# Half of a normalised input brought in transposed and scaled by GpSimd, in a gated feed-forward kernel

## The chip, the cores and the metric

The kernel runs on one core of a Trainium2 chip. The metric is the device time of one launch in microseconds; less is better. All data are fp32.

## The reference

The input has 2 x 1024 = 2048 tokens of 512 features. It is layer-normalised once, and the result goes through two branches:

```python
xn = (x - mean) / sqrt(var + 1e-5)                 # per token
s  = xn @ (weight * (block mask > 0)).T            # 512 -> 512, mask by blocks of 32 x 32
nx = xn * rsqrt(mean(xn**2) + 1e-5) * ln_w         # per token, per feature
f  = (silu(nx @ gate_w.T) * (nx @ up_w.T)) @ down_w.T   # 512 -> 1792 -> 512
out = x + s * silu(f)
```

## The kernel before, in words

**Layout.** The kernel works on transposed data: features on the 128 partitions, 512 tokens (a token tile, t = 0 to 3) on the free axis. The normalised input is thus a grid of blocks (c, t), with c = 0 to 3 the block of 128 features. All large tiles are slots of 128x512 in one SBUF tensor `mem`; `RINGS` gives names to stretches of it (B1 to B7, v5, tmp, free and so on), and `F` their first slots.

**Fast matrix products, twice nested.** The grid is split in two by two (K is the half of the features, H the half of the tokens), and each such block again in two by two (k, n). Both levels use a Winograd-like scheme with seven products in place of eight. An outer product q needs sums or differences of outer blocks: `outer_b` makes them for q = 5, 6, 7 and 4 (for 1, 2 and 3 a block is used as it is). `inner_b` makes the same sums within the blocks of q. On the side of the weights `inner_a` does it on GpSimd. An instance j is one outer product of one group of weights g (seven groups of gate and up columns, and an eighth for the masked linear); it consists of seven inner products m, each a matmul of 128x128x512 that PE runs as two records. An instance starts at position 7j of the order.

**Banks.** The products of an instance accumulate in PSUM banks x, y and z, and the running sum of a bank is read between two products of the same bank (`snap` and `total`, DVE for the instances with a prior, ACT for many of the others). Of instance j, DVE's read `total x` stands at position 7j + 9, and the product m=4, which goes on in the same bank x, at 7j + 12.

**The order.** Nothing is scheduled by a tool. Each step is put in a list with a position, `at(pos, fn, ...)`; the list is sorted by position and issued under a manual schedule, so that every engine works through its own share of it in that order. One position is about the length of one product. The first 16 instances (positions 0 to 112) are q = 1 and 2 of all groups, which need only the first token half (t = 0 and 1). From position 112 on the instances use the other five outer products, which need the second half too. The blocks of the second half are therefore made ready beside the running instances, at positions 40 to 118.

**The second half before.** Token tiles 2 and 3 are loaded with tokens on the partitions. `stats` and `factors` give for each token a scale and a shift (`scl`, `nb`). `normalise` applies them in place, four times on ACT for t = 2 and four times on DVE for t = 3. Then PE transposes them, for each (t, c) four 128x128 transposes into one bank of the ring V. For c = 2 and 3 ACT copies the bank to SBUF (`evacuate`); for c = 0 and 1 `outer_b` reads the bank itself, once for q = 5 and once for q = 7. `outer_b` for q = 6 and `inner_b` read two SBUF tiles. The subtractions of `outer_b` are on DVE, except those for q = 4, which are on GpSimd (POOL).

**What else runs there.** `mask_rows` are four reductions on DVE at positions 62 to 72.5. DVE multiplies gate and up values (`h_out`), ACT evaluates silu. POOL makes the weight sums `inner_a(g, 1)` of group g at position 14g − 7 and the following three; group 6 has its products m=5, 6, 3 and 7 at positions 86, 88, 90 and 92. The queue of SP issues nearly all transfers, in the order of the list. The factors of the RMS norm already go through a small tensor in DRAM: `rms_store` transposes them with PE, copies them, and stores them with one transfer; `rms_rows` later loads each row of 512 tokens, broadcast to 128 partitions.

Of the kernel before, what the change touches and what calls it, by code (L numbers as in the profile page):

```python
# [8 lines left out]
F32 = mybir.dt.float32  # L9
I32 = mybir.dt.int32  # L10
AF = mybir.ActivationFunctionType
ALU = mybir.AluOpType
AX = mybir.AxisListType

P = 128
W = 512
# [15 lines left out]
def tile_masked_linear_gated_ffn(  # L32
# [11 lines left out]
    nc = tc.nc  # L44
    NT, H = x.shape
    KC = H // P
    G = gu.shape[0]
    NTT = NT // W
    TT = W // P
# [2 lines left out]
    h_dram = tc.dram_tile([7, G, 2, P, W], F32, name="h_dram")  # L52
    s_dram = tc.dram_tile([KC, NTT, P, W], F32, name="s_dram")
    rms_dram = tc.dram_tile([NT], F32, name="rms_dram")
    acc_dram = tc.dram_tile([G + 1, P, 4, W], F32, name="acc_dram")
    dw_dram = tc.dram_tile([4, P, G, 256], F32, name="dw_dram")

    const = ctx.enter_context(tc.tile_pool(name="const", bufs=1))
    small = ctx.enter_context(tc.tile_pool(name="small", bufs=2))
# [8 lines left out]
    def at(pos, fn, *args):  # L68
        events.append((pos, len(events), fn, args))
# [5 lines left out]
    mem = big.tile([P, sum(n for _, n in RINGS), W], F32, tag="mem", name="mem")  # L75
# [5 lines left out]
    F = first_slot  # L81

    def slot(tag, name=None):
        i, n = ring[tag]
        ring[tag][0] += 1
        return mem[:, first_slot[tag] + i % n, :]
# [6 lines left out]
    def bank(tag, name):  # L93
        return ps.tile([P, W], F32, tag=tag, name=name, bufs=PSB[tag])

    def add(eng, o, a, b, op=ALU.add):
        eng.tensor_tensor(o, a, b, op)  # L97

    dve, pool, act = nc.vector, nc.gpsimd, nc.scalar
# [3 lines left out]
    ident = const.tile([P, P], F32, tag="ident", name="ident")  # L103
# [9 lines left out]

    xt, raw, stat = {}, {}, {}
    agg = small.tile([P, NTT, TT, 2], F32, tag="agg", name="agg", bufs=1)
    rms = small.tile([P, NTT, TT], F32, tag="rms", name="rms", bufs=1)

    def load_x(t):
# [10 lines left out]
    def factors(t):  # L129


        scl = small.tile([P, TT], F32, tag="scl", name=f"scl_{t}")
        nb = small.tile([P, TT], F32, tag="nb", name=f"nb_{t}")
        stat[t] = (scl, nb)

        def last():
            nc.vector.reciprocal(scl, scl)
            nc.vector.scalar_tensor_tensor(nb, agg[:, t, :, 0], -1.0, scl, ALU.mult, ALU.mult)

        return [lambda: nc.vector.tensor_scalar(scl, agg[:, t, :, 1], 1.0 + EPS, EPS * EPS, ALU.mult, ALU.add),  # L140
                lambda: nc.scalar.activation(scl, scl, AF.Sqrt), last]
# [8 lines left out]
    pt = {}  # L150
# [17 lines left out]
    def rms_factor():  # L168

        def first():  # L170
            nc.vector.tensor_scalar_add(rms, agg[:, :, :, 1], EPS)
            nc.vector.reciprocal(rms, rms)
            nc.vector.tensor_mul(rms, agg[:, :, :, 1], rms)
            nc.vector.tensor_scalar_add(rms, rms, EPS)
        return [first, lambda: nc.scalar.activation(rms, rms, AF.Sqrt)]

    def rms_store():

        b = bank("V", "rms_rows")
        nc.tensor.transpose(b[: NTT * TT, :P], rms.rearrange("p t i -> p (t i)"), ident)  # L180
        rows = small.tile([NTT * TT, P], F32, tag="rms_rows", name="rms_rows", bufs=1)
        nc.vector.tensor_copy(rows, b[: NTT * TT, :P])
        nc.sync.dma_start(rms_dram.rearrange("(i p) -> i p", p=P), rows)

# [4 lines left out]
        nc.sync.dma_start(rms_bc[t], rms_dram[t * W : (t + 1) * W].unsqueeze(0).to_broadcast([P, W]))  # L189


    bblk, bop = {}, {}

    def outer_b(q, k, n, eng):


        B = lambda K, H_: pt[2 + n, k] if (K, H_) == (0, 1) else raw[2 * K + k, 2 * H_ + n]
        if q in (1, 2, 3):
            bblk[q, k, n] = B(*{1: (0, 0), 2: (1, 0), 3: (1, 1)}[q])
            return  # L200
        o = mem[:, F["free"], :] if (q, k, n) == (4, 0, 1) else slot("tmp" if (k, n) == (0, 1) else f"B{q}")
        a, b = {
            5: lambda: (B(0, 1), B(0, 0)),
            6: lambda: (B(1, 1), bblk[5, k, n]),
            7: lambda: (B(1, 1), B(0, 1)),
            4: lambda: (B(1, 0), bblk[6, k, n]),
        }[q]()
        add(eng, o, a, b, ALU.subtract)
        bblk[q, k, n] = o
# [274 lines left out]
    K3 = G // 2  # L484
# [55 lines left out]
    def first_h(q, k, i5, i7):  # L540

        st = {}

        def in_bank():
            st[0] = bank("V", f"h_{k}")
            nc.scalar.copy(st[0], dh[q][:, 1, k, :])

        def sums():
            for m, i in ((5, i5), (7, i7)):
                dt.setdefault((q, m), slots(i, K3))  # L550
            add(dve, dt[q, 5][:, k, :], st[0], dh[q][:, 0, k, :], ALU.subtract)
            add(dve, dt[q, 7][:, k, :], dh[q][:, 1, K3 + k, :], st[0], ALU.subtract)

        return in_bank, sums
# [119 lines left out]
    where = {gq: j for j, gq in enumerate(order)}  # L674
    N = len(order)
    END = 7 * N
# [16 lines left out]
    def plan(pos, step, todo):  # L693
        for i, fn in enumerate(todo):
            at(pos + step * i, fn)
# [32 lines left out]
    for i in range(TT):  # L728
        at(14.0 + 2.5 * i, stats, 2, i)
        at(25.0 + 3 * i, stats, 3, i)  # L730
        at((44.0, 51.0, 55.2, 58.2)[i], normalise, 2, i, act)
        at(40.5 + 2.4 * i, normalise, 3, i, dve)
    plan(36.2, 1.2, rms_factor())

    for t, p0 in ((3, 51.5), (2, 65.5)):
        n = t % 2
        for k, c in enumerate((2, 3, 0, 1)):
            for i in range(TT):
                at(p0 + 2 * k + 0.01 * i, transpose, t, c, i, "V")
            if c >= 2:  # L740
                at(p0 + 2 * k + 1.2, evacuate, t, c, act)
            else:
                at(p0 + 2 * k + 1.2, outer_b, 5, c, n, dve)
                at(p0 + 2 * k + 1.21, outer_b, 7, c, n, dve)
    for k in (0, 1):
        for n in (0, 1):
            at(72, outer_b, 3, k, n, None)
    for n, p0 in ((1, 60), (0, 74)):
        for k in (0, 1):
            at(p0 + 1.5 * k, outer_b, 6, k, n, dve)  # L750
            at(p0 + 2.2 + 1.7 * k + (16 if n == 1 else 4), outer_b, 4, k, n, pool)
    for q, p in ((6, 77), (5, 83), (4, 89), (7, 100), (3, 118)):
        for off, m, eng in ((0, 5, dve), (3, 6, dve), (5.5, 7, pool), (7.5, 4, pool)):
            at(p + off, inner_b, q, m, eng)

# [2 lines left out]
    for g in range(G + 1):  # L758
        p, rest = 7 * where[g, 1], 7 * where[g, BLOCKS[0]]
# [40 lines left out]
    free = [p for p in range(END, END + 25 * 7 + 20) if p not in taken]  # L800
    DOWN = (1, 2, 6, 5, 7, 3, 4)

    def D(o):
        return lambda k: free[25 * o + k] if 25 * o + k < 25 * len(DOWN) else free[25 * o + k - 1] + 1
# [1 line left out]
    H0, H1 = F["B1"], F["B6"]  # L806
    TS = [F["B7"] + K3 * k for k in range(5)]
    first_t = {5: F["q"] - 1, 7: F["vc"], 6: F["a1"], 4: TS[1]}
    b11, b12, b21, b22, e0, e1 = (0, 0, K3), (1, 0, K3), (0, K3, 2 * K3), (1, K3, 2 * K3), (0, G - 1, G), (1, G - 1, G)
    QD, later = (F["a1"] + 4, F["acc"], F["s"] + 5), {}  # L810
    for o, q in enumerate(DOWN):
        if o == 0:
            parts = [(p, 7 * where[min(k, 4) + 1, 6] + 11) for k, p in enumerate((b11, b12, b22, b21, e0, e1))]
        elif o == 1:
            parts = [(p, END - 22 + 7 * p[0]) for p in (b11, b21, e0, b12, b22, e1)]
        else:
            d = D(o - 2)
            parts = [(b11, d(4)), (b12, d(4) + 0.1), (b21, d(14)), (b22, d(21)), (e0, d(25) + 1), (e1, d(25) + 1.1)]
        for part, pos in parts:
            at(pos, load_h, q, (H0, H1)[o % 2], part)  # L820
        for k, m in enumerate((5, 6, 7, 4)):
            if o:
                at(D(o - 1)((3, 8, 12, 18)[k]) + 0.3, inner_h, q, m, TS[(4 * o + k + 3) % 5])
            elif m in (6, 4):
                at(END + {6: -1.95, 4: 7.5}[m], inner_h, q, m, first_t[m])
        if o == 0:
            for k in range(K3):
                in_bank, sums = first_h(q, k, first_t[5], first_t[7])
                at(END - 24.4 + 7 * k, in_bank)
                at(END - 22.95 + 7 * k, sums)  # L830
        at((END - 29.8, END - 14, END + 7)[o] if o < 3 else D(o - 2)(4), load_d, q, QD[o % 3])

        def weight_sums(q=q, i=F["q"] + 2 - 3 * (o % 2), o=o):
            for k, fn in enumerate(inner_d(q, i)):
                later[o, k] = fn
        for k in range(4):
            pos = END + (-6, -4.8, 2, 4)[k] if o == 0 else D(o - 1)(10) + 2.5 * k
            if k == 0:
                at(pos, weight_sums)
            at(pos, lambda o=o, k=k: later[o, k]())  # L840
# [81 lines left out]
```

## Time and profile before

| | us |
|---|---|
| time, median of 3 runs | 514.32 (514.15 to 514.35) |
| profiled execution, its own time | 514.33 |
| span of its profile | 512.5 |
| busy in that span: PE, DVE, POOL, ACT | 506.2, 380.8, 340.5, 181.7 |
| 128x512 on DVE, a PSUM and an SBUF operand | 0.68 each |
| 128x512 on POOL, two SBUF operands | 1.27 each |
| granted clock of PE | 1.0 |

The span is the time from the first to the last recorded instruction; 1.8 us of the execution lie around it. A row of a timeline gives the start and the length in us, the engine, the line of the kernel, the operation, out<-in, and how many instructions were merged in it; in brackets stands how long the engine had been idle, and what ended that. PEld is the weight load, which runs ahead of its matmul. Line 97 is the helper `add`, through which all sums and differences go. Consecutive DVE instructions of 128x512 start 0.60 us apart.

### The profile page before, as it was taken

The numbers are of one execution on the slowest core, as the hardware profiler recorded it, in microseconds if no ns is written. First come the engines' busy times: TensorE is split into PE (matmuls) and PEld (weight loads), VectorE is DVE, ScalarE is ACT, GpSimd is POOL, SyncE is SP. The second block draws the span as 40 slices with busy tenths as digits, with TensorE's granted clock in tenths as the row PEclk, the third lists the DMA queues.
The fourth block names the chain that finished last, engine by engine and source line by source line (L and its number), as shares of the span: only waits on it lengthen the run. The fifth ranks groups of instructions, "written<-read, shape, count | busy, mean of one in ns | idle before, by whom it ended". The sixth has DMA issues, their size and how long they took to land. (4 is left out here: it accounts for less than half of the span.)

```text
span 512.5 us, 4939 instructions
## 1 busy us (share of the span) xinstructions
PE 506.2 (99%) x1277; PEld 231.2 (45%) x1277; DVE 380.8 (74%) x586; ACT 181.7 (35%) x344; POOL 340.5 (66%) x282
## 2 busy tenths in 40 slices
PE   8999999999999999999999999999999999999997
PEld 7444444444444444444444444444444444444444
DVE  5879689875987969789696978968847645367736
ACT  3566864642536344353634433331100101001111
POOL 5522223994695978869598789977652664739960
PEclk9999999999999999999999999999999999999999
DMA  8335645359159486685948567499997698467372
GB/s 310 142 123 215 245 156 217 153 226 329 60 220 334 165 297 233 230 299 209 315 181 296 205 246 258 156 334 390 352 345 269 198 382 320 146 255 220 145 230 83
DMA packets 60460, 121.59 MB, mean 237 GB/s; under 512 B 5760, under 2 KB 13328, under 8 KB 58384
## 3 DMA queue, kind: packets, MB, share of 16 engines
q1 hardware_dynamic: 60144, 120.75, 66.1%
q10 hardware_dynamic: 288, 0.52, 0.3%
q8 instruction: 10, 0.16, 0.1%
q14 instruction: 18, 0.15, 0.1%
HBM read 75.11 MB, written 46.15 MB: 237 GB/s over the span
## 5 line engine op out<-in xcount | busy, mean ns | idle before, releaser
L97 POOL TENSOR_TENSOR mem<-mem 128x512 f32<-128x512 f32 (+4 forms) x245 | 305.8, 1270 | 136.7 <-ACT mem L264 37.6
L343 PE MATMUL x<-mem 128*128 128x512 f32 x448 | 213.6, 594 | 0.3
L343 PEld LDWEIGHTS x<-mem 128*128 128x128 f32 x448 | 83.7, 190 | 106.9 <-issue 86.7
L97 DVE TENSOR_TENSOR mem<-x,mem 128x512 f32<-128x512 f32 x137 | 92.6, 684 | 42.2 <-PE x L343 41.1
L343 PE MATMUL y<-mem 128*128 128x512 f32 x224 | 114.6, 593 | 0.7 <-DVE mem L97 0.7
L97 DVE TENSOR_TENSOR mem<-mem 128x512 f32<-128x512 f32 (+3 forms) x60 | 75.6, 1266 | 7.2 <-PE dx L591 4.4
L591 PE MATMUL dx<-mem 128*128 128x512 f32 x174 | 78.3, 592 | 0.0
L97 DVE TENSOR_TENSOR mem<-y,mem 128x512 f32<-128x512 f32 x96 | 65.7, 684 | 10.0 <-PE y L343 8.7
L343 PEld LDWEIGHTS y<-mem 128*128 128x128 f32 x224 | 42.2, 190 | 53.3 <-issue 46.7
L350 ACT COPY z<-x 128x512 f32<-128x512 f32 x54 | 30.9, 573 | 97.8 <-PE x L343 93.3
L343 PE MATMUL z<-mem 128*128 128x512 f32 x112 | 57.1, 593 | 0.0
L591 PEld LDWEIGHTS dx<-mem 128*128 128x128 f32 x174 | 33.1, 190 | 41.6 <-issue 40.9
L591 PE MATMUL dy<-mem 128*128 128x512 f32 x98 | 44.5, 592 | 0.0
L409 ACT ACTIVATE gate<-mem 128x512 f32<-128x512 f32 x56 | 33.1, 601 | 25.4 <-DVE mem L97 21.0
L414 DVE TENSOR_TENSOR mem<-gate,mem 128x512 f32<-128x512 f32 x56 | 38.1, 681 | 5.1 <-POOL mem L97 4.3
L564 POOL TENSOR_TENSOR mem<-mem 128x512 f32<-128x512 f32 x16 | 24.3, 1516 | 15.4 <-DMA mem<-s_dram 15.1
L343 PEld LDWEIGHTS z<-mem 128*128 128x128 f32 x112 | 21.0, 190 | 25.3 <-issue 24.4
L574 ACT ACTIVATE silu<-mem 128x512 f32<-128x512 f32 x15 | 9.0, 602 | 64.6 <-DVE mem L97 48.3
L97 DVE TENSOR_TENSOR mem<-z,mem 128x512 f32<-128x512 f32 x41 | 28.0, 682 | 3.4 <-PE z L343 3.4
L591 PEld LDWEIGHTS dy<-mem 128*128 128x128 f32 x98 | 18.6, 190 | 23.4 <-issue 23.2
L97 DVE TENSOR_TENSOR mem<-dx,mem 128x512 f32<-128x512 f32 x16 | 11.0, 690 | 20.1 <-PE dx L591 20.1
L591 PE MATMUL dz<-mem 128*128 128x512 f32 x56 | 25.2, 592 | 0.0
(72 smaller groups left out, 286.8 us busy)
## 6 DMA issues: line engine op xcount, KB each, us to landing
h_dram<-mem SPq DMA_DIRECT2D x98, 256.0 KB, 2.1
mem<-h_dram SPq DMA_DIRECT2D x28, 768.0 KB, 6.7
mem<-in_gu SPq DMA_DIRECT2D x42, 256.0 KB, 4.0
acc_dram<-mem SPq DMA_DIRECT2D x8, 1024.0 KB, 4.1
mem<-acc_dram SPq DMA_DIRECT2D x8, 1024.0 KB, 6.0
s_dram<-mem SPq DMA_DIRECT2D x16, 256.0 KB, 4.4
mem<-s_dram SPq DMA_DIRECT2D x16, 256.0 KB, 6.7
mem<-in_x_t SPq DMA_DIRECT2D x16, 256.0 KB, 6.4
```

The costliest lines, as they stand in the source:

```text
L97: eng.tensor_tensor(o, a, b, op)
L343: nc.tensor.matmul(st[key], weights(g, q, m), operand(q, m), start=first and not (key == "z" and seeded), stop=True, skip_group_check=True)
L350: nc.scalar.copy(st["z"], st["x"])
L409: nc.scalar.activation(gate[key], t(), AF.Silu)
L414: nc.vector.tensor_mul(a(), gate[key], b())
L564: at_later.append(lambda: nc.gpsimd.tensor_tensor(s_tile, s_tile, rms_bc[t], ALU.mult))
L574: nc.scalar.activation(b[0][:, part], y[:, part] if source is None else source(), AF.Silu)
L591: nc.tensor.matmul(st[key], w(), b(), start=first and key != "z", stop=True, skip_group_check=True)
```

## The change

Token tiles 2 and 3 are loaded a second time, now from the transposed copy of the input in DRAM (`x_t`), so that features lie on the partitions at once (`load_xt`, eight transfers). Their scale and shift then vary along the free axis. So the factors of both tiles are gathered in one small tile `fac`, transposed once by PE, stored in a small DRAM tensor (`fac_rows`), and loaded back as four rows that are broadcast to 128 partitions (`fac_load`). POOL multiplies each of the eight blocks by the scale row and adds the shift row, in place (`scale_xt`, 16 instructions). The 32 transposes, the eight `normalise` and the four `evacuate` of the second half go. The subtractions `outer_b` for q = 5 and 7 now read two SBUF tiles. Positions of `outer_b` and `inner_b` change, and some slots.

```diff
+    fac_dram = tc.dram_tile([NT], F32, name="fac_dram")
...
+    fac = small.tile([P, 2, 2, TT], F32, tag="fac", name="fac", bufs=1)
...
+        if t < 2:
+            scl = small.tile([P, TT], F32, tag="scl", name=f"scl_{t}")
+            nb = small.tile([P, TT], F32, tag="nb", name=f"nb_{t}")
+        else:
+            scl, nb = fac[:, t - 2, 0, :], fac[:, t - 2, 1, :]
...
+    def load_xt(t, c):
+        K, k, n = c // 2, c % 2, t % 2
+        v = mem[:, F["v5"] + 4 + 2 * n + k, :] if K == 0 else slot("tmp" if (k, n) == (0, 1) else "B3")
+        (b12 if K == 0 else raw)[(k, n) if K == 0 else (c, t)] = v
+        nc.sync.dma_start(v, x_t[c * P : (c + 1) * P, t * W : (t + 1) * W])
+
+    def fac_rows():
+        b = bank("V", "fac_rows")
+        nc.tensor.transpose(b[: 4 * TT, :P], fac.rearrange("p t f i -> p (t f i)"), ident)
+        rows = small.tile([4 * TT, P], F32, tag="rows", name="fac_sb")
+        nc.vector.tensor_copy(rows, b[: 4 * TT, :P])
+        nc.sync.dma_start(fac_dram.rearrange("(i p) -> i p", p=P), rows)
+
+    def fac_load(t):
+        for f in range(2):
+            i = 2 * (t - 2) + f
+            fac_bc[t, f] = mem[:, F["B6"] + 3 + i, :]
+            nc.sync.dma_start(fac_bc[t, f], fac_dram[i * W : (i + 1) * W].unsqueeze(0).to_broadcast([P, W]))
+
+    def scale_xt(t, c, f):
+        v = b12[c, t % 2] if c < 2 else raw[c, t]
+        add(pool, v, v, fac_bc[t, f], (ALU.mult, ALU.add)[f])
...
-        B = lambda K, H_: pt[2 + n, k] if (K, H_) == (0, 1) else raw[2 * K + k, 2 * H_ + n]
+        B = lambda K, H_: b12[k, n] if (K, H_) == (0, 1) else raw[2 * K + k, 2 * H_ + n]
...
-        at((44.0, 51.0, 55.2, 58.2)[i], normalise, 2, i, act)
-        at(40.5 + 2.4 * i, normalise, 3, i, dve)
...
-    for t, p0 in ((3, 51.5), (2, 65.5)):
-        n = t % 2
-        for k, c in enumerate((2, 3, 0, 1)):
-            for i in range(TT):
-                at(p0 + 2 * k + 0.01 * i, transpose, t, c, i, "V")
-            if c >= 2:
-                at(p0 + 2 * k + 1.2, evacuate, t, c, act)
-            else:
-                at(p0 + 2 * k + 1.2, outer_b, 5, c, n, dve)
-                at(p0 + 2 * k + 1.21, outer_b, 7, c, n, dve)
+    for k, (t, c) in enumerate((t, c) for t in (3, 2) for c in range(KC)):
+        at(21.0 + 2 * k, load_xt, t, c)
+        for f in range(2):
+            at((53.5 if t == 3 else 67.5) + 3 * c + 1.5 * f, scale_xt, t, c, f)
+    at(41, fac_rows)
+    for t in (3, 2):
+        at(41.5, fac_load, t)
...
-    for n, p0 in ((1, 60), (0, 74)):
-        for k in (0, 1):
-            at(p0 + 1.5 * k, outer_b, 6, k, n, dve)
-            at(p0 + 2.2 + 1.7 * k + (16 if n == 1 else 4), outer_b, 4, k, n, pool)
-    for q, p in ((6, 77), (5, 83), (4, 89), (7, 100), (3, 118)):
+    for n, p0 in ((1, 61.05), (0, 75.05)):
+        for off, q, k in ((0, 5, 0), (0.01, 5, 1), (7, 7, 0), (7.01, 6, 0), (9.25, 7, 1), (10.25, 6, 1)):
+            at(p0 + off, outer_b, q, k, n, dve)
+        for k in (0, 1):
+            at(p0 + 11.5 + 1.5 * k, outer_b, 4, k, n, pool)
+    for q, p in ((6, 88), (5, 94), (7, 102), (4, 110), (3, 120)):
         for off, m, eng in ((0, 5, dve), (3, 6, dve), (5.5, 7, pool), (7.5, 4, pool)):
             at(p + off, inner_b, q, m, eng)
```

More of the change, by code (lines that the diff above doesn't have):

```diff
@@ L129, in factors @@
     def factors(t):
-        scl = small.tile([P, TT], F32, tag="scl", name=f"scl_{t}")
-        nb = small.tile([P, TT], F32, tag="nb", name=f"nb_{t}")
+        if t < 2:
[3 more added lines that the diff above has]
+            scl, nb = fac[:, t - 2, 0, :], fac[:, t - 2, 1, :]
         stat[t] = (scl, nb)
@@ L180, in rms_store @@
         nc.tensor.transpose(b[: NTT * TT, :P], rms.rearrange("p t i -> p (t i)"), ident)
-        rows = small.tile([NTT * TT, P], F32, tag="rms_rows", name="rms_rows", bufs=1)
+        rows = small.tile([NTT * TT, P], F32, tag="rows", name="rms_rows")
         nc.vector.tensor_copy(rows, b[: NTT * TT, :P])
@@ L189, in rms_rows @@
         nc.sync.dma_start(rms_bc[t], rms_dram[t * W : (t + 1) * W].unsqueeze(0).to_broadcast([P, W]))
+    b12, fac_bc = {}, {}
+    def load_xt(t, c):
[17 more added lines that the diff above has]
+        add(pool, v, v, fac_bc[t, f], (ALU.mult, ALU.add)[f])
     bblk, bop = {}, {}
     def outer_b(q, k, n, eng):
-        B = lambda K, H_: pt[2 + n, k] if (K, H_) == (0, 1) else raw[2 * K + k, 2 * H_ + n]
+        B = lambda K, H_: b12[k, n] if (K, H_) == (0, 1) else raw[2 * K + k, 2 * H_ + n]
         if q in (1, 2, 3):
@@ L200, in outer_b @@
             return
-        o = mem[:, F["free"], :] if (q, k, n) == (4, 0, 1) else slot("tmp" if (k, n) == (0, 1) else f"B{q}")
+        o = mem[:, F["v5"] + 8, :] if (q, k, n) == (4, 0, 1) else slot("tmp" if (k, n) == (0, 1) else f"B{q}")
         a, b = {
@@ L730, in tile_masked_linear_gated_ffn @@
         at(25.0 + 3 * i, stats, 3, i)
-        at((44.0, 51.0, 55.2, 58.2)[i], normalise, 2, i, act)
-        at(40.5 + 2.4 * i, normalise, 3, i, dve)
     plan(36.2, 1.2, rms_factor())
-    for t, p0 in ((3, 51.5), (2, 65.5)):
-        n = t % 2
-        for k, c in enumerate((2, 3, 0, 1)):
-            for i in range(TT):
-                at(p0 + 2 * k + 0.01 * i, transpose, t, c, i, "V")
-            if c >= 2:
-                at(p0 + 2 * k + 1.2, evacuate, t, c, act)
-            else:
-                at(p0 + 2 * k + 1.2, outer_b, 5, c, n, dve)
-                at(p0 + 2 * k + 1.21, outer_b, 7, c, n, dve)
+    for k, (t, c) in enumerate((t, c) for t in (3, 2) for c in range(KC)):
[5 more added lines that the diff above has]
+        at(41.5, fac_load, t)
     for k in (0, 1):
         for n in (0, 1):
-            at(72, outer_b, 3, k, n, None)
-    for n, p0 in ((1, 60), (0, 74)):
+            at(82, outer_b, 3, k, n, None)
+    for n, p0 in ((1, 61.05), (0, 75.05)):
+        for off, q, k in ((0, 5, 0), (0.01, 5, 1), (7, 7, 0), (7.01, 6, 0), (9.25, 7, 1), (10.25, 6, 1)):
+            at(p0 + off, outer_b, q, k, n, dve)
         for k in (0, 1):
-            at(p0 + 1.5 * k, outer_b, 6, k, n, dve)
-            at(p0 + 2.2 + 1.7 * k + (16 if n == 1 else 4), outer_b, 4, k, n, pool)
-    for q, p in ((6, 77), (5, 83), (4, 89), (7, 100), (3, 118)):
+            at(p0 + 11.5 + 1.5 * k, outer_b, 4, k, n, pool)
+    for q, p in ((6, 88), (5, 94), (7, 102), (4, 110), (3, 120)):
         for off, m, eng in ((0, 5, dve), (3, 6, dve), (5.5, 7, pool), (7.5, 4, pool)):
@@ L808, in tile_masked_linear_gated_ffn @@
     first_t = {5: F["q"] - 1, 7: F["vc"], 6: F["a1"], 4: TS[1]}
-    b11, b12, b21, b22, e0, e1 = (0, 0, K3), (1, 0, K3), (0, K3, 2 * K3), (1, K3, 2 * K3), (0, G - 1, G), (1, G - 1, G)
+    p11, p12, p21, p22, e0, e1 = (0, 0, K3), (1, 0, K3), (0, K3, 2 * K3), (1, K3, 2 * K3), (0, G - 1, G), (1, G - 1, G)
     QD, later = (F["a1"] + 4, F["acc"], F["s"] + 5), {}
@@ L812, in tile_masked_linear_gated_ffn @@
         if o == 0:
-            parts = [(p, 7 * where[min(k, 4) + 1, 6] + 11) for k, p in enumerate((b11, b12, b22, b21, e0, e1))]
+            parts = [(p, 7 * where[min(k, 4) + 1, 6] + 11) for k, p in enumerate((p11, p12, p22, p21, e0, e1))]
         elif o == 1:
-            parts = [(p, END - 22 + 7 * p[0]) for p in (b11, b21, e0, b12, b22, e1)]
+            parts = [(p, END - 22 + 7 * p[0]) for p in (p11, p21, e0, p12, p22, e1)]
         else:
             d = D(o - 2)
-            parts = [(b11, d(4)), (b12, d(4) + 0.1), (b21, d(14)), (b22, d(21)), (e0, d(25) + 1), (e1, d(25) + 1.1)]
+            parts = [(p11, d(4)), (p12, d(4) + 0.1), (p21, d(14)), (p22, d(21)), (e0, d(25) + 1), (e1, d(25) + 1.1)]
         for part, pos in parts:
```

## The prediction

> **What bounds the kernel now.** I read the page first: busy time by engine, then the slices, then the busy time in ten-microsecond windows, then the timelines of the stage that the change touches.
>
> ```profile
> PE 506.2 (99%) x1277; PEld 231.2 (45%) x1277; DVE 380.8 (74%) x586; ACT 181.7 (35%) x344; POOL 340.5 (66%) x282
> ```
>
> TensorE (PE) is busy for 506 of 512.5 us. From 30 us on it has next to no idle time, so work taken off PE shortens the run one for one, provided that no other engine becomes late for it. The windows show who has room where the change works (columns: PE, PEld, DVE, ACT, POOL busy us):
>
> ```profile
> 50.00:60.00 10.00, 10.00 (x28) 4.62 (x27) 7.43 (x13) 8.68 (x16) 1.64 (x3) 1.00 0.57 217
> 60.00:70.00 10.00, 10.00 (x33) 4.97 (x32) 7.72 (x13) 6.72 (x13) 1.24 (x2) 1.00 0.64 238
> 70.00:80.00 10.00, 10.00 (x37) 5.18 (x36) 8.04 (x14) 4.45 (x9) 2.88 (x4) 1.00 0.47 169
> 80.00:90.00 10.00, 10.00 (x26) 4.58 (x25) 9.80 (x18) 4.93 (x10) 5.12 (x6) 1.00 0.55 191
> 90.00:100.00 10.00, 10.00 (x25) 4.42 (x24) 8.45 (x13) 6.03 (x14) 10.00 (x8) 1.00 0.46 184
> ```
>
> GpSimd (POOL) has some 20 us of idle time between 50 and 85 us. VectorE (DVE) has not: 8 of 10 us, then 9.8. The price of the transposes is in PE's timeline:
>
> ```profile
> 52.87 1.02 PE L343 MATMUL z<-mem 128*128 128x512 f32 x2
> ...
> 58.02 1.02 PE L343 MATMUL y<-mem 128*128 128x512 f32 x2
> 58.88 0.60 PE L155 MATMUL pt<-ident,mem 128*128 128x128 f32 x4
> 59.31 1.02 PE L343 MATMUL z<-mem 128*128 128x512 f32 x2
> ```
>
> From 58.02 to 58.88 is one product (two records, 0.858 us), from 58.88 to 59.31 four transposes: 0.43 us. The z product at 52.87 stands at position 45 of the written order, so without the later transposes position p falls at 14.26 + 0.858 p us.
>
> What decides the case is a pair of rows further on, where POOL is busy while DVE subtracts two SBUF tiles (POOL's rows each from a window of its own):
>
> ```profile
> 86.29 1.27 POOL L97 TENSOR_TENSOR mem<-mem 128x512 f32<-128x512 f32 x1
> 87.52 1.18 POOL L97 TENSOR_TENSOR mem<-mem 128x256 f32<-128x256 f32 x1
> ...
> 86.93 1.17 DVE L97 TENSOR_TENSOR mem<-mem 128x512 f32<-128x512 f32 x1
> 88.03 0.68 DVE L97 TENSOR_TENSOR mem<-y,mem 128x512 f32<-128x512 f32 x1
> ```
>
> DVE's subtraction takes 1.17 us in place of 0.68: it ends at 88.10, so it really ran from 87.42, when POOL's instruction ended. POOL's next one takes 1.18 in place of 0.73: it waited 0.45 us. I looked up the five such DVE instructions between 86 and 98 us: each time POOL pays about 0.45 us (0.73 to 1.18 twice, 1.27 to 1.78, 1.72 and 1.73), and DVE waits for the end of POOL's current instruction (0.49, 0, 0, 0.53 and 0.29 us). The row with a PSUM operand (y) takes 0.68 whatever POOL does.
>
> **What the Trainium skill says.** SBUF — State Buffer, "Who interferes with whom": a VectorE instruction with two SBUF inputs contends with a GpSimd instruction that reads SBUF, and the later one is blocked for the whole instruction; one with at most one SBUF input does not. The five cases above agree. GPSIMD Engine Reference, "Performance versus the Vector engine": a two-input fp32 elementwise operation takes GpSimd about twice as long as VectorE. The trace agrees: 1.27 against 0.68 us.
>
> **The change, part by part.**
>
> PE: 32 transposes go, eight sets of 0.43 us: −3.44. One transpose of the factors is added; its twin for rms_rows has 128 columns like the others, so 0.43/4 = +0.11. It stands at position 41 (49.4 us), its input is ready at 48.96 (end of the last L138 row); its weight load wants it some 0.25 us ahead, so 0 to 0.3 of wait; I take +0.15. PE net: −3.2.
>
> ACT loses four normalisations (0.8 each) and four PSUM copies (0.59). It was not late; counted at nothing, and scale_a of group 4 comes 0.8 us sooner, so POOL is free at 60.3 instead of 61.2.
>
> DVE loses four normalisations (0.54) near 50 us, gains one copy (0.28). The eight subtractions that read a transposed bank, and the four for q=6, remain, but now all twelve have **two SBUF inputs**.
>
> SP and DMA: eight x_t loads of 256 KB at positions 21 to 35 (about 32 to 45 us), where the DMA share is 0.22 to 0.64; needed after 60 us, so free. The factor rows: copy done about 50.5, store 2.1 (as the h_dram stores) to 3.4 us (as rms_dram), four loads issued 0.32 apart, landing 3.4 to 6.3 us later (as mem<-rms_dram). The first two are there at 56 to 60.5 us, POOL wants them at 60.3 and 61.6: just hidden. SP waits for the store up to 3.4 us; behind it stand an acc_dram store and an h_dram store whose buffers are wanted a round later, and two gu loads, wanted 5 us after they land. Free.
>
> POOL gains 16 instructions of 128x512 (1.23 apart, 1.35 where one waits for its predecessor): 16 x 1.23 + 5 x 0.12 = 20.3 us. By length they fit into the idle time. They also keep POOL busy without a gap from 60.3 to past 95 us, and that is the cost: every outer subtraction of DVE now meets a running POOL.
>
> Follow DVE around position 72 (instance 9). In the trace it reads bank x at 75.01 (position 68); five transpose sets lay before that, so now 75.01 − 2.15 + 0.11 = 72.97. The queue behind it is now: q=7, q=6, mask_rows, total y, q=7, q=6, and then the read of x at position 72. The last product of this instance (m=4) accumulates into the same bank and must wait for that read; it starts at 82.13 − 3.44 + 0.11 = 78.8. A subtraction directly behind another waits for one POOL instruction between them: 1.23 + 0.45 = 1.68 from start to start. Let w be the wait of the first of each pair:
> 72.97 + 0.60 + w + 1.68 + 0.60 + 0.60 + 0.60 + w + 1.68 + 0.60 + 0.68 = 80.0 + 2w.
> With w from 0 to 1.23 I take the middle, 0.6, since POOL now runs without gaps (the five cases above had 0 to 0.53). The bank is free at 81.2; PE wants it at 78.55 (0.25 ahead). Stall: 2.7 us (1.5 to 3.9). Before, the same read ended at 80.0 for a product at 82.1: 2 us in hand.
>
> The second half repeats it at position 82 to 89 without the mask: the product at position 81 starts at 14.26 + 0.858 x 81 + 0.11 = 83.87, DVE reads x 1.06 later as in the trace, at 84.93 + 2.7; then 0.60 + w + 1.68 + 0.60 + 0.60 + w + 1.68 + 0.60 + 0.68: free at 94.1 + 2w, wanted at 90.5 + 2.7 = 93.2. Stall 0.9 + 1.2 = 2.1 us (0.9 to 3.4). Its first operands come from POOL: 17 instructions, 4 sums and ten waits of 0.45 put the last scaled tile near 90, in time for it. The pairs at positions 61 and 75 have the reads of later products behind them with 2 us in hand: I add 0.3.
>
> The inner_b steps go 2 to 21 positions later, on DVE and POOL, and two of the four POOL outer_b earlier. Their first result is wanted by the product at position 114; POOL's queue from 90 us on (two outer_b, two masks, eight inner_b, eight weight sums, 25 us) ends at 115, where it ended at 118 before. Counted at nothing; without that cover each microsecond would be one of PE.
>
> Sum: −3.44 + 0.11 + 0.15 + 2.7 + 2.1 + 0.3 = +1.9. From 105 us on the order is as before and PE is busy, so nothing is given back. The profiled execution took 514.33 us (span 512.5 and 1.8 around it), 0.01 from the median: **516.2 us**.
>
> **The rivals.**
> - *Only POOL pays* (the subtractions slip in between POOL's instructions, w near 0 and no wait within pairs). Then DVE is in time, but POOL's sums for group 6 (wanted at position 86, 88.1 less 0.25) come after 17 x 1.23 + 0.6 + 5 x 0.7 + 10 x 0.45 from 60.3, at 89.8: stall 1.9. 514.33 − 3.2 + 1.9 = 513.0. For it: two of the five cases did not wait. Against: pairs stand back to back. 0.15.
> - *All hidden*, the other side: POOL's idle 20 us take the 20.3 us and DVE's 2 us in hand absorb the waits. 514.33 − 3.2 = 511.1. It decides if the summed waits of DVE's four subtractions stay below about 1.3 us. Against: five of five cases. 0.13.
> - *Rows late*: DRAM rows land after 62 us; each microsecond moves POOL's whole chain and, through operands that DVE waits for, the second stall: about 517.5 to 518.5. For it: the four rms_dram loads took up to 6.3 us. 0.07.
> - That the transposes stay is excluded by the diff.
>
> **How the numbers follow.** The forecast has 0.65, with its own range 514.8 to 518.2 (w between its ends, in both rounds not at once). What can be told from no change is 0.2%, 1.03 us. Faster: all hidden 0.13 and half of "only POOL" 0.07: 0.20. Same: the other half 0.08 and the foot of the forecast 0.06: 0.14. Slower: 0.59 + 0.07 = 0.66. The range leaves out "all hidden" and the top: 512.2 to 518.2.
>
> **What would show it.** PE's busy time falls by about 3.3 us in the sum of its instructions while idle time of 4 to 5 us appears between 76 and 95 us, put down to DVE as the releaser of x products; DVE mem<-mem rows near 1.2 us and POOL rows near 1.7 in that stretch. The forecast is wrong if DVE's subtractions stay at 0.68 beside a busy POOL, if PE has no gap there, or if the gaps are released by POOL or a DMA.

## The result, and the profile after

| | before | after |
|---|---|---|
| time, median of 6 runs each, us | 514.21 (513.99 to 514.35) | 515.99 (515.67 to 516.42) |
| ratio after to before, 95% interval | | 1.0035 (1.0024 to 1.0046) |
| span of the profile, us | 512.5 | 514.2 |
| TensorE, from its first steady z product to its last matmul, us | 479.96 | 480.47 |
| from DVE's last instruction to the end of the span, us | 2.62 | 3.89 |

The changed kernel is 1.8 us slower; 516.2 was forecast. The last two rows split the loss: 0.51 us of it lies in TensorE's stream, and 1.27 us after the last arithmetic, where the forecast had nothing. (In the two profiles the first steady product also comes 0.17 us earlier after the change. Some expectations below have 3.93 and 1.35 us for these ends; they were worked out with spans rounded to 0.1 us.)

In the profile of the changed kernel `add` is line 98, the products of the instances are line 374, and the stores of the output line 609. Its page has this line of busy time:

```profile
PE 504.5 (98%) x1246; PEld 228.4 (44%) x1246; DVE 385.2 (75%) x583; ACT 176.2 (34%) x336; POOL 368.4 (72%) x298
```

PE has 31 instructions fewer and POOL 16 more. DVE has three instructions fewer and is busy 4.4 us longer: its instructions became longer. Busy time in ten-microsecond windows (PE, PEld, DVE, ACT, POOL) shows where:

```profile
60.00:70.00 10.00, 10.00 (x25) 4.39 (x24) 7.68 (x11) 6.02 (x12) 9.77 (x8) 1.00 1.02 394
70.00:80.00 10.00, 9.21 (x22) 3.89 (x21) 9.95 (x15) 4.31 (x9) 9.83 (x9) 1.00 0.34 137
80.00:90.00 10.00, 10.00 (x25) 4.24 (x24) 10.00 (x15) 2.88 (x6) 9.93 (x8) 1.00 0.58 186
90.00:100.00 10.00, 8.47 (x20) 3.37 (x19) 9.34 (x14) 5.53 (x12) 9.84 (x9) 1.00 0.44 176
```

Between 60 and 90 us POOL went from 1 to 5 us of each window to nearly all of it (from 90 us on it was full before too), DVE is nearly full from 70 us on, and PE, full before, has gaps between 70 and 80 and between 90 and 100 us. They lie at these products (PE's timeline of the changed kernel):

```profile
76.84 1.02 PE L374 MATMUL z<-mem 128*128 128x512 f32 x2
77.70 1.02 PE L374 MATMUL x<-mem 128*128 128x512 f32 x2
79.51 1.12 PE L374 MATMUL x<-mem 128*128 128x512 f32 x2 [0.79 <-DVE mem L98]
80.48 1.02 PE L374 MATMUL y<-mem 128*128 128x512 f32 x2
...
90.53 1.02 PE L374 MATMUL z<-mem 128*128 128x512 f32 x2
91.92 1.12 PE L374 MATMUL x<-mem 128*128 128x512 f32 x2 [0.38 <-POOL mem L98]
94.20 1.13 PE L374 MATMUL x<-mem 128*128 128x512 f32 x2 [1.16 <-ACT mem L402]
```

The ends of matmuls are modelled, so these gaps understate the loss. I measure it by the distance from one z product to the next, 6.01 us for an instance without a stall. On that scale 1.06 us are lost between 76.84 and 84.08 (0.17 for the mask's product taken off), 0.44 in the next instance, 2.06 between 90.53 and 98.60, and 0.36 between 104.61 and 110.98: 3.9 us. On the same scale the transposes had cost the kernel before 3.51 us (its four instances from 52.87 to 80.41), and the transposition of the factors costs 0.11; the balance is the 0.5 of the table.

The gap before 94.20 is put down to ACT, whose copy ended at 94.16. But that copy reads bank z, and the product goes on in bank x, which DVE had just read; the row of the product's own weight load, also at 94.20, names DVE. DVE's timeline of the changed kernel, around both stalls:

```profile
72.75 0.69 DVE L98 TENSOR_TENSOR mem<-x,mem 128x512 f32<-128x512 f32 x1
73.36 2.02 DVE L98 TENSOR_TENSOR mem<-mem 128x512 f32<-128x512 f32 x2
75.31 0.67 DVE L331 TENSOR_REDUCE mask_sums<-mem 128x16 f32<-128x512 int32 x1
75.91 0.67 DVE L98 TENSOR_TENSOR mem<-y,mem 128x512 f32<-128x512 f32 x1
76.50 2.35 DVE L98 TENSOR_TENSOR mem<-mem 128x512 f32<-128x512 f32 x2
78.78 0.68 DVE L98 TENSOR_TENSOR mem<-x,mem 128x512 f32<-128x512 f32 x1
...
91.22 2.33 DVE L98 TENSOR_TENSOR mem<-mem 128x512 f32<-128x512 f32 x2 [0.56 <-POOL mem L98]
93.47 0.68 DVE L98 TENSOR_TENSOR mem<-x,mem 128x512 f32<-128x512 f32 x1
```

The read of x ends at 79.46, the product starts at 79.51; it ends at 94.15, the product starts at 94.20. Ahead of each read stand two pairs of subtractions with two SBUF inputs, and these four pairs take 2.0 to 2.35 us where two instructions of 0.68 us, 0.60 apart, take 1.28. (The two pairs of q = 5, at 65.57 and 80.57, take 2.36 and 2.99.) What holds them is seen in POOL's rows (each from a narrow window of its own):

```profile
74.80 1.72 POOL L98 TENSOR_TENSOR mem<-mem 128x512 f32<-128x512 f32 x1
76.59 1.71 POOL L98 TENSOR_TENSOR mem<-mem 128x512 f32<-128x512 f32 x1
78.26 1.73 POOL L98 TENSOR_TENSOR mem<-mem 128x512 f32<-128x512 f32 x1
```

The first subtraction of the pair at 76.50 slips in just before POOL's instruction at 76.59, which then takes 1.71 us where 1.27 is its undisturbed length; the second waits until that one is done at 78.3; then POOL's next waits in its turn. The two engines take turns.

### The profile page after: what moved, and what is told of

Same layout as the page of the kernel before. It is cut to its first block, busy times and chain, and to the rows that moved or that the text cites. A ratio compares the mean times of both kernels' runs of the same rounds, so it can differ in the third digit from the quotient of the medians.

```text
span 514.2 us, 4896 instructions
## 1 busy us (share of the span) xinstructions
PE 504.5 (98%) x1246; PEld 228.4 (44%) x1246; DVE 385.2 (75%) x583; ACT 176.2 (34%) x336; POOL 368.4 (72%) x298
## 5 line engine op out<-in xcount | busy, mean ns | idle before, releaser
L98 POOL TENSOR_TENSOR mem<-mem 128x512 f32<-128x512 f32 (+4 forms) x261 | 332.4, 1296 | 109.4 <-ACT mem L402 32.4
L98 DVE TENSOR_TENSOR mem<-mem 128x512 f32<-128x512 f32 (+2 forms) x68 | 88.2, 1307 | 8.2 <-PE dx L622 4.4
L622 PE MATMUL dx<-mem 128*128 128x512 f32 x174 | 78.3, 592 | 0.0
```

The source lines that it names most:

```text
L622: nc.tensor.matmul(st[key], w(), b(), start=first and key != "z", stop=True, skip_group_check=True)
```

## The experiments

Each ratio is to runs of the kernel before that were taken beside it (median 514.21 us for the changed kernel, 514.39 to 514.56 for the others), so small differences between rows are best read from the ratios and the last two columns. "In PE" is the change of the stretch from the first z product to the last matmul; "end" runs from DVE's last instruction to the end of the span (2.62 us in the kernel before).

| kernel | us | ratio to before (95%) | in PE | end |
|---|---|---|---|---|
| changed kernel | 515.99 | 1.0035 (1.0024 to 1.0046) | +0.51 | 3.89 |
| bank_operand | 513.07 | 0.9970 (0.9959 to 0.9982) | −2.38 | 3.67 |
| pool_writes_only | 514.41 | 0.9999 (0.9991 to 1.0007) | −1.16 | 3.38 |
| no_scale | 512.60 | 0.9962 (0.9948 to 0.9975) | −3.19 | 3.89 |
| reads_first | 516.14 | 1.0032 (1.0019 to 1.0045) | +0.60 | 3.83 |
| bank_first_half | 515.64 | 1.0026 (1.0018 to 1.0035) | +0.16 | 3.72 |
| before_dma | 515.39 | 1.0018 (1.0011 to 1.0025) | +0.02 | 3.60 |
| before_pad | 515.44 | 1.0020 (1.0013 to 1.0026) | +0.01 | 3.65 |
| after_pad | 515.50 | 1.0020 (1.0013 to 1.0027) | +0.54 | 3.14 |
| bank_pad | 512.07 | 0.9952 (0.9939 to 0.9966) | −2.49 | 2.84 |
| bank_merged | 511.90 | 0.9949 (0.9937 to 0.9962) | −2.45 | 2.71 |
| bank_inner_later | 511.31 | 0.9942 (0.9928 to 0.9955) | −3.04 | 2.74 |

### Is it the two SBUF operands?

**bank_operand** gives DVE's outer subtractions a PSUM operand again: ACT copies the first operand to a bank of the ring V.

```diff
+        if eng is dve:
+            if q != 6:
+                obank[k, n] = bank("V", f"ob_{q}_{k}_{n}")
+                nc.scalar.copy(obank[k, n], a)
+            a = obank[k, n]
         add(eng, o, a, b, ALU.subtract)
```

> The changed kernel, but ACT copies one operand of each of DVE's twelve outer subtractions into a PSUM bank first (eight copies), so that DVE reads one SBUF tile only; GpSimd's work is untouched. Shared-read theory: the subtractions take 0.68 us beside a busy GpSimd, GpSimd's rows stay at 1.27, PE's stalls in 75 to 110 us fall from 3.8 to below 1 us, and the time is 511.5 to 512.8, below both kernels. Rival (GpSimd's queue is simply too long and its sums come late): the stalls stay at 3 us or more, 515 to 516.

It took 513.07 us: 1.5 below the kernel before, where the changed kernel is 1.8 above it, and 2.9 of the 3.9 us of stalls in PE are gone. The time is above the range expected for the shared read, because the longer end stayed (3.67 us). In its groups by shape, from 60 to 96 us (count | busy us, mean ns | idle before), the twelve subtractions are:

```profile
L98 DVE TENSOR_TENSOR mem<-ob,mem 128x512 f32<-128x512 f32 x12 | 7.8, 683 | 2.8 <-ACT ob L242 2.7
...
L98 POOL TENSOR_TENSOR mem<-mem 128x512 f32<-128x512 f32 x20 | 25.1, 1271 | 0.4
```

and in the changed kernel:

```profile
L98 DVE TENSOR_TENSOR mem<-mem 128x512 f32<-128x512 f32 x13 | 15.4, 1217 | 0.6 <-POOL mem L98 0.6
...
L98 POOL TENSOR_TENSOR mem<-mem 128x512 f32<-128x512 f32 x19 | 27.3, 1456 | 0.4
```

An operand moved to PSUM takes DVE's instruction from 1217 to 683 ns and POOL's from 1456 to 1271 (the thirteenth of the changed kernel's is a sum of `inner_b`). Neither does less arithmetic, and ACT does eight copies more.

**pool_writes_only** leaves that operand in SBUF and takes away POOL's reads: the 16 scale and shift instructions become fills of the same tiles, two or three for each, so that POOL stays busy for about as long. The second half is thus not scaled.

```diff
-        add(pool, v, v, fac_bc[t, f], (ALU.mult, ALU.add)[f])
+        for _ in range(3 - f):
+            pool.memset(v, 0.5)
```

> The changed kernel, but each of the 16 scale instructions on GpSimd is replaced by two or three fills of the same tile with a constant (the scaling is left out): GpSimd is kept busy about as long and DVE waits for the same instructions, but GpSimd reads nothing meanwhile. Shared-read theory: subtractions beside the fills take 0.68 us, stalls below 1.5 us, 511.5 to 512.8. Rival (length of GpSimd's queue): about as the changed kernel, 515 to 516.

The first stall is gone. DVE's timeline of this kernel shows a pair beside fills without any wait, and a pair beside POOL's weight sums, which still read, with it:

```profile
73.59 2.07 DVE L98 TENSOR_TENSOR mem<-mem 128x512 f32<-128x512 f32 x2
...
76.77 1.28 DVE L98 TENSOR_TENSOR mem<-mem 128x512 f32<-128x512 f32 x2
...
89.66 2.33 DVE L98 TENSOR_TENSOR mem<-mem 128x512 f32<-128x512 f32 x2 [1.06 <-POOL mem L222]
```

So it is not that POOL is busy, but that it reads. This agrees with the Trainium skill (SBUF — State Buffer, "Who interferes with whom"): a VectorE instruction with two SBUF inputs contends with GpSimd instructions that read SBUF, and not with those that only write it. The last row shows a second cost, which stays here: a fill that comes late from POOL's queue keeps DVE idle for 1.06 us, and the instance at 89.60 loses 1.44 us. With it some 2.1 us of stalls are left, more than the 1.5 expected, and the time, 514.41 us, lies between the ranges of the two theories: the reads explain the first stall, and the length of POOL's queue has a share in the second.

### What the work itself costs

**no_scale** leaves the 16 instructions out, so the second half enters unscaled; loads, factors and the order stay.

```diff
-        for f in range(2):
-            at((53.5 if t == 3 else 67.5) + 3 * c + 1.5 * f, scale_xt, t, c, f)
```

> The changed kernel with the 16 scale instructions left out (the second half is not normalised); everything else as it is. Both theories: no waits, PE stalls below 0.5 us; it measures what the rest of the change is worth: by my sum -3.44 + 0.11 + 0.15 on PE, 511.1. If the end of the run is longer by 1.3 us whatever PE does, as the changed kernel's trace shows after its last matmul, 512.4.

PE's stretch is 3.19 us shorter than before; the prediction's sum without its stalls was 3.18. What it counted at nothing (ACT, the normalisations gone from DVE, the later `inner_b`) sums to about 0.2 us here. The time fell by less, 2.0 us, because the long end remained, as the expectation's second figure had it.

### Can the order help?

**reads_first** puts the second pair of each half behind the read of x that PE waits for.

```diff
-        for off, q, k in (..., (9.25, 7, 1), (10.25, 6, 1)):
+        for off, q, k in (..., (10.96, 7, 1), (10.97, 6, 1)):
```

> The changed kernel, but the second pair of DVE's subtractions in each half (q=7 and q=6 for k=1) stands just behind the read of bank x (positions 72 and 86) in place of ahead of it. If only the place in DVE's queue is at fault: the stall of 1.07 us at 78 us and most of that at 93 us go, 513.5 to 514.5. If it is the amount of DVE's waiting that counts: the stall comes back at the next read of a bank, 79 positions in, and the time stays at 515 to 517.

The time did not change. The instance at 77.36 takes 6.18 us, so the first stall is gone, but the pair now delays the next read of x, in PE's timeline of this kernel:

```profile
86.53 1.13 PE L374 MATMUL x<-mem 128*128 128x512 f32 x2 [1.05 <-DVE mem L98]
```

It costs 1.5 us there, and 0.4 to 0.9 in each of the four instances after it. DVE's queue is full; a moved wait is paid at the next read.

**bank_first_half** is bank_operand for the blocks of n = 1 only (positions 61 to 71), to see whether the first stall feeds the second.

```diff
-        if eng is dve:
+        if eng is dve and n == 1:
```

> As bank_operand, but only the six subtractions of the first half (token tile 3) get a bank operand; those of tile 2 read two SBUF tiles as in the changed kernel. Shared-read theory: the stall of 1.07 us at 78 us goes, the stalls between 84 and 95 us (2.2 us in the changed kernel) stay or shrink a little, since GpSimd's queue starts the second half 1.5 to 2 us sooner; PE net of the kernel before -2 to -1, time 513.2 to 514.5. If the stalls of the second half are an after-effect of the first: as bank_operand, 513.

The time missed its range. The first stall shrinks to 0.22 us, but PE gains only 0.35 over the changed kernel. The two instances of the second stall lose 0.53 and 1.71 us where they lost 0.44 and 2.06, so it shrinks only a little, as expected; but the two instances from 97.77 to 110.80 lose 0.17 and 0.85 where they lost nothing and 0.36. PE's timeline of this kernel names the reader that the changed kernel's row had put down to ACT:

```profile
93.37 1.13 PE L379 MATMUL x<-mem 128*128 128x512 f32 x2 [1.44 <-DVE mem L98]
```

Each half makes its own stall: the second is no after-effect of the first. Of the 0.84 us gained at the first, about half is lost again further on, where `inner_b` works beside a busy POOL; why it loses more there than in the changed kernel was not followed up.

### The longer end

Nothing that the change touches stands near the end, yet DVE's last instruction there is followed by 3.89 us rather than 2.62. **before_dma** adds to the kernel before only the change's transfers: eight loads of `x_t` into slots that are not yet in use, one small store and four broadcast loads of rows of ones.

```diff
+    for k, (t, c) in enumerate((t, c) for t in (3, 2) for c in range(KC)):
+        at(21.0 + 2 * k, extra_xt, t, c)
+    at(41, extra_rows)
+    for i in range(4):
+        at(41.5, extra_load, i)
```

> The kernel before, with the thirteen transfers of the change added (eight x_t loads, one store and four broadcast loads of factor rows, here of constants) at the same positions; nothing uses them. If the new transfers delay anything inside the run, PE gets gaps and the time rises by 1 us or more with PE's last matmul later. If they are hidden but bring the longer end (1.35 us more from DVE's last instruction to the end of the span), PE ends as before and the time is 515.4 to 515.9. If they do neither: 514.2 to 514.6.

PE's stretch is unchanged to 0.02 us and the end is 0.98 us longer. **before_pad** asks whether it is their bytes: thirteen transfers of the small vector `ln_w` instead.

```diff
+    for i in range(13):
+        at(21.0 + i, lambda i=i: nc.sync.dma_start(pads[:, i, :], ln_w))
```

> The kernel before with thirteen transfers of 2 KB added on SP's queue early in the run, so only the number of SP's instructions is that of the changed kernel. If the longer end comes from the number of instructions on that queue: as before_dma in its end, 515.4 to 515.9. If it comes from what is transferred: 514.2 to 514.6.

The same 1.0 us come, with next to no bytes. What they share is thirteen more instructions in SP's stream, more than 450 us ahead of the place where the time is lost. SP's queue at the last stores shows it. The kernel before (each row from a window of its own):

```profile
509.47 0.40 SPq L578 DMA_DIRECT2D out<-mem  x1
509.97 0.41 SPq L578 DMA_DIRECT2D out<-mem  x1
```

before_pad:

```profile
509.06 0.39 SPq L579 DMA_DIRECT2D out<-mem  x1
509.87 0.33 SPq L579 DMA_DIRECT2D out<-mem  x1
```

The changed kernel:

```profile
509.35 0.37 SPq L609 DMA_DIRECT2D out<-mem  x1
510.13 0.33 SPq L609 DMA_DIRECT2D out<-mem  x1
510.57 0.39 SPq L609 DMA_DIRECT2D out<-mem  x1
```

One of the distances between neighbouring issues is 0.78 to 0.81 us where the kernel before has 0.50 at most, and the stores then also land later (median of the last four 2.4 us from issue in the changed kernel, 2.0 in the kernel before).

Three kernels move SP's stream by other counts. **bank_merged** is bank_operand with eight loads of `x_t` made into six (the blocks of c = 0 and 1 of a token tile together) and the four rows loaded by two.

```diff
+        if K == 0:
+            if k == 1:
+                nc.sync.dma_start(slots(i, 2), x_t[: 2 * P, ...].rearrange("(k p) w -> p k w", p=P))
+            return
...
+        nc.sync.dma_start(rows, fac_dram[i * W : (i + 2) * W].unsqueeze(0).to_broadcast([P, 2 * W]))
```

> bank_operand with four transfers less: two x_t blocks in one load where their slots adjoin, and the scale and shift row of a token tile in one load. PE as in bank_operand. If the end depends on the number of SP's instructions it may change by up to 1.3 us, so 511.7 to 513.1; otherwise 513.0.

**bank_pad** and **after_pad** add sixteen transfers like those of before_pad to bank_operand and to the changed kernel.

```diff
+    for i in range(16):
+        at(21.0 + i, lambda i=i: nc.sync.dma_start(pads[:, i, :], ln_w))
```

> bank_operand with sixteen transfers of 2 KB added on SP's queue early. PE as in bank_operand. If the place of SP's last instructions within its instruction stream sets the end, the end moves (2.5 to 4 us) and the time with it, 511.7 to 513.5; if any added transfer prolongs it, it is 3.6 us or more and 513.1 or above.

> The changed kernel with sixteen transfers of 2 KB added on SP's queue early, as in bank_pad. The end of the run (from DVE's last instruction) should be about 2.8 us as in bank_pad, in place of 3.93; PE's stalls stay at 3.7 us. Then the time is about 1.1 us less than the changed kernel's, 514.7 to 515.2, and the part of the loss that the stalls make beyond the saving is only 0.5 us.

With four transfers fewer bank_operand's end falls from 3.67 to 2.71 us, and with sixteen more from 3.67 to 2.84. SP's queue in bank_pad:

```profile
507.02 0.41 SPq L615 DMA_DIRECT2D out<-mem  x1
507.52 0.40 SPq L615 DMA_DIRECT2D out<-mem  x1
```

after_pad takes 0.75 us off the changed kernel's end, about 0.4 less than I expected, and its time, 515.5, is above the range I gave. The long distance is gone from its last stores too (0.50 us at most), but the last two still land 2.4 and 2.1 us after their issue, where the kernel before has 1.9 and 1.7.

The traces have 590 instructions of SP in the kernel before and 601 in bank_merged (short end), 603 in before_dma and before_pad and 604 in the changed kernel and bank_operand (long end), and 620 in bank_pad (short again) and after_pad (between). So the number of transfers is not itself the cost. Followed one by one, these instructions show what is: in all thirteen traces SP stands still for 0.34 us or more ahead of its 80th, 208th, 336th and 464th instruction, and in the twelve that have one ahead of its 592nd. That is a pause at every 128th; at the 592nd it is 0.34 to 0.35 us each time, where an instruction that has nothing to wait for follows the one before it within 0.03 to 0.06. The kernel before ends two short of the 592nd. In the four kernels named with a long end the pause falls between the last stores; in bank_merged it falls just behind the last one, where SP waits for the landings anyway; in bank_pad and after_pad it has passed some 20 us earlier.

The pause is only part of the longer end. In the changed kernel the last store is issued 0.30 us after DVE's last instruction rather than 0.04, it takes 2.56 us to land rather than 1.74, and 1.03 us follow rather than 0.84. Why the stores land later is not shown. Nor is the reason of the pause: a fetch of instructions would fit, and the traces do list such fetches, of 8 KB each, but they start anywhere from 0.6 to 2.9 us after the pause at the 592nd.

### A version that beats both

bank_merged still loses 0.6 us where the `inner_b` pairs of q = 5 and 7 meet a read of x (101.2 to 107.8 us). **bank_inner_later** moves them.

```diff
-    for q, p in ((6, 88), (5, 94), (7, 102), (4, 110), (3, 120)):
+    for q, p in ((6, 88), (5, 100), (7, 107), (4, 113), (3, 120)):
```

> bank_merged with the inner sums of q=5, 7 and 4 six, five and three positions later (100, 107, 113), so that DVE's queue has less to do between positions 94 and 104. bank_merged has 0.6 us of stall between 101 and 108 us there. If DVE's load at that place makes it, it goes and the time is 511.3 to 511.6; if not, 511.9.

It took 511.31 us: 0.58% below the kernel before (0.45 to 0.72%), and the largest stall left in this stage is 0.22 us, between 76.98 and 83.38. That is the prediction's sum without the stalls, to 0.2 us. The transposes were worth taking off PE; what cost more was the form of the operands left behind.

## Why the prediction was right, and where it was not

- **PE's saving**: predicted −3.18 with a wait of 0.15 for the factors. The transposition of the factors started without a wait, and the instance around it (46.69 to 52.81) is 0.11 longer, as costed. no_scale measured −3.19. That the two agree so well is in part chance: the transposes had cost 3.51 rather than 3.44, the +0.15 did not come, and no_scale still loses 0.19 in the instance at 89.42.
- **ACT, SP, DMA and the later `inner_b` at nothing**: shown for ACT and the transfers inside PE's stretch by no_scale and before_dma. For `inner_b` it does not hold while DVE is full: the instance at 104.61 loses 0.36 us, and bank_inner_later wins back the 0.6 us that bank_merged loses at this place.
- **The mechanism** (two SBUF inputs, POOL busy with reads, the read of bank x behind two pairs): bank_operand and pool_writes_only show it from both sides, and the gaps lie within the 76 to 95 us that were named. They are smaller than named, 2.3 us of recorded idle time in place of 4 to 5, and one of the three, 0.38 us, is POOL's.
- **First stall**, predicted 2.7, measured 1.06. The term that failed is w, the wait of the first of a pair: 0.6 was put in twice, as the middle of 0 to 1.23. It was 0.2 at 73.36 and about 0 at 76.50: 1.0 us less. The instruction between the first pair was a sum of 256 columns, 1.13 us from start to start where 1.68 was put in: 0.5 less. DVE came to bank x 0.22 us sooner. Over the six pairs of the changed kernel w was 0, 0.2, 0, 0.6, 0.4 and 0.5, so 0.6 was the top of what occurred and not its middle.
- **Second stall**, predicted 2.1, measured 2.06, with 0.44 in the instance ahead of it, where 0.3 was added for the pairs at positions 61 and 75. The sizes agree, the terms do not. From the read at 87.21 to the end of the read at 93.47 DVE took 6.9 us where the sum had 7.6. Here w was 0.4 and 0.5, near its 0.6; but between the two of each pair POOL again had a sum of 256 columns, 1.13 us from start to start where 1.68 was put in: 1.1 less. Against that, 0.64 are not contention at all but a wait for an operand that POOL had not yet made (DVE's row at 91.22): the last scaled tile, put "near 90, in time", came at 91.2. And since the first stall was 1.6 us shorter than predicted, PE also wanted the bank about 1 us sooner. PE's row at 91.92 waits for a sum of POOL for group 6. So a part of the rival "Only POOL pays" is true: POOL's queue, stretched by the turns it loses, is itself late, by 0.5 us for PE where that rival had 1.9.
- **The end**: predicted "nothing is given back" after 105 us. PE did give nothing back, but the end grew by 1.27 us. before_dma reproduces 0.98 of it with transfers that were rightly costed at nothing in their own stage.

The sum thus agreed partly by cancelling: 3.9 us of stalls instead of 5.25 with the small wait, and 1.27 us at an end that was counted as fixed. The sign and the mechanism stand on experiments; the closeness to 516.2 does not.

## What to carry to other kernels

When work moves to GpSimd, go through VectorE's instructions in that stretch and count those with two SBUF inputs: each can cost up to the length of GpSimd's current instruction (0 to 1.2 us here), both engines pay (GpSimd 0.45 us for each turn lost), and a PSUM copy of one operand made by an idle ScalarE removes it. A free window on the receiving engine is not yet room: look for the next PSUM read in VectorE's queue that TensorE waits for, and at how much time it has in hand. Before the gain or loss of a change is put down to its stage, split it into that stage and the end of the run.

## What the runs showed of the hardware that was not expected

SP pauses for 0.34 us or more ahead of every 128th instruction of its stream, in all thirteen traces. Where the 592nd fell among the last stores, the last 3 us of the run were 1.0 to 1.3 us longer. Thirteen small transfers issued at about 30 to 45 us brought it there (before_pad), and sixteen more on top of a similar count moved it out again (bank_pad, after_pad). The end of a run of this length can thus vary by 0.2% for a reason that has nothing to do with the work near it. Why the stores land later there was not settled.

A pair of back-to-back subtractions beside a reading GpSimd takes 2.0 to 3.0 us against 1.28 beside fills. In each of the six pairs of the changed kernel exactly one instruction of GpSimd ran between the two: from the end of one subtraction to the end of the next it is about 1.68 us where GpSimd's instruction had 512 columns, and 1.13 to 1.14 where it had 256. The engines alternate, so the wait of the second can be worked out from what GpSimd runs at that moment; only the first one's wait is open, and it was 0 to 0.64 us.
